# Dilated attention and a depthwise convolution on one core: the first image's loads put first, and the last image's convolution in an order of its own with diagonal products on TensorE

## The chip, the cores and the metric

The kernel runs on one core of a Trainium2 chip. The metric is the device time of one execution in microseconds (us); a change of the time by less than about 0.2% can't be told from none. Engines are named as the profile names them: PE is TensorE (its weight loads are PEld), DVE is VectorE, ACT is ScalarE, POOL is GpSimd and SP is SyncE, which here only issues transfers.

## The reference

The input is 16 images of 56 x 56 pixels with 384 channels, in single precision. Two residual layers are computed, each on a group normalisation with 32 groups of 12 channels:

```python
def _dilate_attention(q, k, v, head_dim, kernel, dil):
    ...
    attn = jnp.einsum('bgdn,bgdkn->bgnk', qg, ku) * scale
    attn = jax.nn.softmax(attn, axis=-1)
    out = jnp.einsum('bgnk,bgdkn->bgnd', attn, vu)
...
# --- layer 0 (conv_preact) ---
x = x + _L0_conv_ref(_gn(x), L0_conv_w_qkv, L0_conv_w_proj, L0_conv_b_proj)
# --- layer 1 (conv_preact) ---
x = x + _L1_conv_ref(_gn(x), L1_conv_w)
```

Layer 0 projects to q, k and v, splits the channels into 3 groups of 128 (4 heads of 32) with dilation 1, 2 and 3, lets every pixel attend to its 3 x 3 dilated neighbours, and projects back. Layer 1 is a depthwise 3 x 3 convolution with weights of -1, 0 or 1.

## The kernel before

**Chunks.** An image is worked in 7 chunks of 8 rows (448 pixels), channels on the partitions in three tiles of 128. There are N = 112 chunks, and each passes three stages. `plan_a` (L489) loads x, turns it with TensorE transposes (L510), copies it out on ACT (L523), takes statistics on DVE (L525) and stores it as `xd`. `plan_b` (L544) is layer 0: it normalises, projects (L562), scores (L627 on DVE, L608 on PE), takes the softmax, weighs (`weigh`, L686: products on DVE at L706, sums over neighbours on POOL at L716, 128 x 1344 elements each), and projects out (L737), then takes the statistics of the result (L747) and stores it as `x1d` (L750). `plan_c` (L774) is layer 1 and writes the output.

**Layer 1** treats its three channel tiles differently. Tile 0 (`column(0)` and `convolve(0)`): ACT writes the centre tap and an offset into a PSUM bank (L850), and DVE adds the eight other taps, one instruction each (L874). Tile 1: ACT likewise, but six taps are done by PE as eight products of diagonal matrices with three rows stacked on 96 partitions (L863), and two taps stay on DVE. Tile 2 (`taps_g`, `sum_g`): ACT multiplies nine times (L937), POOL adds (L947, L952, L955). For the last image alone tile 2 runs wholly on DVE instead, in nine instructions (`taps_last`, L928). Then `turn` (L958) transposes the chunk back on PE (L964), ACT copies (L970) and a transfer stores it (L973).

**Statistics.** The convolution of an image can't start before the statistics of its whole layer 0 are there. `group_norm` (L375) is a chain from DVE to PE to DVE to PE to DVE to POOL to PE to DVE to POOL to PE to DVE, with a yield at each handover. It is run for layer 0 of image 0 at the very start, and for layer 1 of image 15 at the end.

**What sets the order.** Every piece of work is filed under a number (`at`, `put`), in units where a chunk is 9 steps (`STEP`); pieces are emitted in the order of these numbers, read from the table `WHEN`. `pin` ties each instruction to the one before it on its engine while `FROM <= when < UNTIL`, that is from 81 to 1022. Outside of this stretch a scheduler fills in instructions as it thinks them ready, in emission order where it has a choice. So both ends of the program, the first image's loads and all that is filed at 1022 or later (the last image's convolution with the four chunks of image 14 before it), are ordered by the scheduler. The start files the x loads under -200 (`FIRST`), the projection weights under the same number on ACT's queue (`load_weights`, L251), and the turning of these weights between the chunks of x (`turn_qkv_weights`, L288). The small weights come in twelve transfers of single 4-byte elements and one of the bias, on SP's queue (L275, L277, L284). Constants for selections and padding are built on POOL before anything else, and a PE product of two of them (`pz`, L221) stands ahead of the transposes on PE.

**Buffers around the change.** x of image 0 is loaded into one `xin` buffer and two `z` buffers, so three chunks are under way at once. In layer 1 the tiles 0 and 1 of a chunk lie in `x1` (two buffers); a buffer comes free when `turn` has transposed it, and the next load into it is issued on SP (L835).

Of the kernel before, what the change touches and what calls it, by code (L numbers as in the profile page):

```python
# [17 lines left out]
P = 128  # L18
# [48 lines left out]
C_SHIFT = 0  # L67
FIXED_ENGINES = ("PE", "DVE", "Activation", "Pool", "SP")
# [3 lines left out]
def dilated_attention_then_binary_conv(  # L72
# [61 lines left out]
    nc.gpsimd.memset(sel, 0.0)  # L134
    for h in range(HEADS):
        nc.gpsimd.memset(sel[h * HD : (h + 1) * HD, SEL0 + h : SEL0 + h + 1], 1.0)


    perm = const.tile([P, NPAD, HEADS], F32, name="perm")
    nc.gpsimd.memset(perm, 0.0)  # L140
    for p in range(NPAD):

        v = place(p) if p < NG * NTAP else p
        nc.gpsimd.affine_select(
            out=perm[:, v, :], in_=perm[:, v, :], compare_op=ALU.not_equal, fill=1.0,
            base=-(32 * (p % 4) + 4 * (p // 4)), pattern=[[-1, HEADS]], channel_multiplier=1,
        )
# [20 lines left out]
    nc.gpsimd.memset(own, 1.0)  # L168
    for lo, s in ((-GN_G, 1), (GN_G + 3, -1)):
        nc.gpsimd.affine_select(  # L170
            out=own, in_=own, compare_op=ALU.is_ge, fill=0.0, base=lo, pattern=[[-4 * s, PARTS]], channel_multiplier=s,
        )
# [36 lines left out]
    nc.gpsimd.memset(to_pack, 0.0)  # L209
    for q in range(NQ):  # L210
        g0, c0, own_rows = (CB * NQ + q) * HD // GN_CH, GN_G + 4 * q, slice(q * HD, (q + 1) * HD)
        for g in range(NG):
            nc.gpsimd.tensor_copy(gsel[:, g, c0 : c0 + 4], gsel[:, g, g0 : g0 + 4])
        nc.gpsimd.tensor_copy(packed[own_rows, c0 : c0 + 4], gsel[own_rows, CB, g0 : g0 + 4])
    for q in range(P // HD):
        nc.gpsimd.affine_select(
            out=fold, in_=fold, compare_op=ALU.not_equal, fill=1.0, base=-q * HD,
            pattern=[[0, P // HD], [-1, HD]], channel_multiplier=1,
        )
    pz = ps_mt.tile([P, 512], F32, tag="mt", name="pz")  # L220
    nc.tensor.matmul(pz[:, :P], packed, fold.rearrange("p a c -> p (a c)"), start=True, stop=True)  # L221
    nc.vector.tensor_copy(gselz, pz[:, :P])
# [3 lines left out]
    for which, slots in enumerate((K_SLOTS, V_SLOTS)):  # L226
        kv.append([])
        for g, d in enumerate(DIL):
            kv[which].append([])
            for s in range(slots):  # L230
                t = const.tile([P, ROWS + 2 * d, W + 2 * d], F32, name=f"{'kv'[which]}_{g}_{s}")
                nc.gpsimd.memset(t[:, :, 0:d], 0.0)
                nc.gpsimd.memset(t[:, :, W + d : W + 2 * d], 0.0)
                kv[which][g].append(t)
# [3 lines left out]
    nc.gpsimd.memset(ew, 0.0)  # L238
    nc.gpsimd.memset(e3, 0.0)


    zg = []
    for s in range(2):
        t = const.tile([P, ROWS + 2, W + 2], F32, name=f"zg_{s}")
        nc.gpsimd.memset(t, 0.0)
        zg.append(t)


    raw = {}

    def load_weights():  # L251
        by_rows = w_qkv.rearrange("(t p) c -> p t c", p=P)
        for k in range(NG):
            raw["q", k] = t = t_p.tile([P, 3, PX], F32, tag="t", name="wq_in")
            nc.scalar.dma_start(t[:, :, :C], by_rows[:, 3 * k : 3 * k + 3, :])
        raw["p"] = t = w_p.tile([P, 3, PX], F32, tag="w", name="wp_in")
        nc.scalar.dma_start(t[:, :, :C], w_proj.rearrange("(t p) c -> p t c", p=P))
# [43 lines left out]
    def small_weights():  # L301
# [15 lines left out]
        nc.vector.tensor_copy(spread, spread_f)  # L317
# [167 lines left out]
    cs1 = {}  # L485
# [3 lines left out]
    def plan_a(m, t0):  # L489
# [17 lines left out]
        def turn(j):  # L507
            pt = ps_mt.tile([P, 512], F32, tag="mt", name="pt_x")
            for s in range(NSUB):
                nc.tensor.transpose(  # L510
                    pt[:, s * SUB : (s + 1) * SUB], had["xin"][:, s, j * P : (j + 1) * P], ident[:SUB, :SUB]
                )
            if b == 0:

                if j == 0:
                    pool, tag = ((xn_p, "xn"), (xn_p, "xn"), (xn_p, "xn"), (xr_p, "xr"), (t_p, "t"), (w_p, "w"),
                                 (w_p, "w"))[c]
                    first[c] = pool.tile([P, NG, PX], F32, tag=tag, name="x_first")
                xa = first[c][:, j]
            else:  # L520
                xa = xa_p.tile([P, PX], F32, tag="xa", name="xa")
            yield
            nc.scalar.copy(xa, pt[:, :PX])  # L523
            yield
            nc.vector.bn_stats(stats0[b][:, j, c, :], xa)  # L525
            yield
            if b:
                nc.sync.dma_start(xd[b][j * P : (j + 1) * P, c * PX : (c + 1) * PX], xa)
            elif j == NG - 1:
                nc.scalar.dma_start(chunk_of(xd[b], c), first[c])  # L530

        if b == 0:
            at(FIRST + 2 * max(c - 2, 0) + .14, load)
            for j in range(NG):
                at(FIRST + 2 * c + 1.11, lambda j=j: [None for _ in turn(j)])
            return
# [7 lines left out]
    def plan_b(m, t0):  # L544
# [141 lines left out]
        def weigh(i):  # L686
# [29 lines left out]
            nc.gpsimd.tensor_tensor(w0, w0, w, ALU.add)  # L716
# [47 lines left out]
    def column_scalars(b):  # L764
# [7 lines left out]
        cs1[b] = cs  # L772

    def plan_c(m, t0):  # L774
# [58 lines left out]
        def load_x():  # L833
            had["x1"] = x1 = x1_p.tile([P, JG, ROWS + 2, W], F32, tag="x1", name="x1")
# [5 lines left out]
        def column(j):  # L840

            x1, cs = had["x1"], cs1[b]
            had["pc", j] = pc = ps_q.tile([P, 512], F32, tag="q", name="pc")
# [11 lines left out]
        def convolve(j):  # L855
# [22 lines left out]

            if j >= CB:
# [3 lines left out]
                yield  # L883
            else:
# [10 lines left out]
        def load_g():  # L895
            if b < B - 1:
# [23 lines left out]
        def taps_last(ky):  # L920
# [4 lines left out]
            acc = rows(had["m"][:, 0])  # L925
            for kx in range(3):
# [48 lines left out]
        if b == B - 1:  # L975

            t0 += max(0, WHEN["statistics"][0][-1] + 1.1 - 36)
            at(t0 - 12 + .14, load_g)
            at(t0 - 3 + .14, load_x)
            ahead = 8 if c > 1 else 1  # L980
            at(t0 - ahead + .13, normalise_g)
            for j in range(JG):
                if j == CB:
                    at(t0 - 12 + j + .14, lambda: [None for _ in load()])
                    at(t0 - ahead + j + .13, lambda: [None for _ in normalise_z()])
                at(t0 + 1 + j + .05, lambda j=j: column(j))
                at(t0 + 1 + j + .05, lambda j=j: [None for _ in convolve(j)])
            for ky in range(3):
                at(t0 + 1 + ky + .05, lambda ky=ky: taps_last(ky))
            for s in range(NSUB):  # L990
                at(t0 + 12.12, lambda s=s: [None for _ in turn(s)])
# [5 lines left out]
        put(t0, "taps", taps_g)  # L997
        put(t0, "sums", lambda n: sum_g(n + 1))
# [10 lines left out]
    FROM, UNTIL = 9 * STEP, STEP * N + 14  # L1009
    at(FIRST + .14, load_weights)  # L1010
    for cc in range(NG):
        at(FIRST + 6 + 2 * cc + .12, lambda cc=cc: turn_qkv_weights(cc))
        at(-21 + cc + .12, lambda cc=cc: turn_proj_weights(cc))
    at(-18 + .14, load_small_weights)
    for o in range(NTAP):
        at(-17 + o + .14, lambda o=o: load_taps(*divmod(o, 3)))
    at(5.14, small_weights)
# [6 lines left out]
    at(FIRST + 8.125, open_banks)  # L1024
# [19 lines left out]
    earliest = min(WHEN["normalise"])[0]  # L1044
    statistics(earliest - 11, [(0, 0)], steps)
    statistics(STEP * NCH + earliest - 3, [(0, 1)], steps)
    for b in range(B):
# [26 lines left out]
    for when in sorted(pieces):  # L1074
        newest["pinned"] = FROM <= when < UNTIL
        for piece in pieces[when]:
            piece()
            pin(FIXED if newest["pinned"] else ())
# [28 lines left out]
```

## Time and profile before

| what | value |
|---|---|
| median of 3 runs | 4941.43 us (4940.76 to 4943.64) |
| the profiled execution, its own time | 4940.53 us |
| its span, first to last instruction | 4938.8 us |
| busy: PE / DVE / POOL / ACT | 4768.9 / 4423.9 / 4226.9 / 2705.6 us |
| mean granted PE clock | 0.978 |
| first projection of layer 0 starts | 56.29 us |
| last statistics input of layer 1 ends (L747) | 4781.2 us |
| statistics of layer 1, image 15, ready (L444) | 4839.8 us |

The page divides the span into 40 slices of 123.5 us; a digit is the busy share of an engine in tenths, and the row PEclk is the clock that PE was granted in tenths of full speed. A row of a timeline is: start, duration, engine, line, operation, out<-in, count, and in brackets the idle time before it and what ended it. The chain of waits is followed back from the last instruction; its rows are start, duration, and what the time went to.

### The profile page before, as it was taken

What the parts mean: (1) busy time and instruction counts of PE and PEld (TensorE: products, weight loads), DVE (VectorE), ACT (ScalarE), POOL (GpSimd) and SP (SyncE); (2) the same over time, 40 slices, a digit from 0 to 9 for tenths busy, and PEclk for the clock granted to TensorE, in tenths of its full rate; (3) what the DMA queues carried; (4) which work ended last, traced back from release to release, by engine and by line L of the source; (5) the groups of instructions that cost most, each with busy time, mean ns of one, the idle gap of its engine ahead of it and who ended that gap; (6) DMA issues with size and microseconds to landing.
All of it is one profiled execution on the core that took longest, in us unless ns stands there. A gap on an engine that the chain in (4) does not pass through costs nothing. (4 is left out here: it accounts for less than half of the span.)

```text
span 4938.8 us, 67211 instructions
## 1 busy us (share of the span) xinstructions
PE 4768.9 (97%) x22571; PEld 2204.8 (45%) x22571; DVE 4423.9 (90%) x4738; ACT 2705.6 (55%) x4952; POOL 4226.9 (86%) x2903
## 2 busy tenths in 40 slices
PE   7999999999999999999999999999999999999954
PEld 4444444444444444444444444444444444444422
DVE  4888899999999999999999999999999999989867
ACT  3332355555555555555555555655555555555565
POOL 2776798999999899998989999899999989999981
PEclk9999999999999999999999999999999999999975
DMA  5433455555555555555555555555555555544454
GB/s 163 131 108 113 134 166 165 161 166 150 166 160 164 164 161 167 153 166 154 164 165 159 168 158 166 165 162 166 150 166 160 164 163 161 160 123 133 120 152 120
DMA packets 765216, 759.93 MB, mean 154 GB/s; under 512 B 356931, under 2 KB 734150, under 8 KB 764870
## 3 DMA queue, kind: packets, MB, share of 16 engines
q1 hardware_dynamic: 756886, 743.64, 53.3%
q10 hardware_dynamic: 7984, 12.00, 0.7%
q8 instruction: 178, 2.92, 0.3%
q14 instruction: 168, 1.38, 0.1%
HBM read 401.27 MB, written 231.21 MB: 128 GB/s over the span
## 5 line engine op out<-in xcount | busy, mean ns | idle before, releaser
L716 POOL TENSOR_TENSOR w<-w 128x1344 f32<-128x1344 f32 x672 | 2050.6, 3051 | 346.1 <-DVE w L706 334.8
L706 DVE TENSOR_TENSOR w<-pb_a,v 128x1344 f32<-128x1344 f32 x1008 | 1557.8, 1545 | 230.2 <-PE pb_a L695 150.7
L627 DVE TENSOR_TENSOR t<-pq,k 128x1344 f32<-128x1344 f32 x1008 | 1513.7, 1547 | 108.9 <-PE pq L562 103.2
L562 PE MATMUL pkv<-xn,wqkvT 128*128 128x448 f32 x3924 | 1584.1, 549 | 2.6 <-DVE var L416 2.6
L562 PEld LDWEIGHTS pkv<-xn,wqkvT 128*128 128x128 f32 x3924 | 719.7, 190 | 673.7 <-issue 630.3
L737 PE MATMUL po<-y,wprojT 128*128 128x448 f32 x2016 | 845.8, 556 | 2.4 <-ACT po L733 2.4
L562 PE MATMUL pq<-xn,wqkvT 128*128 128x448 f32 x1962 | 803.5, 545 | 2.1 <-DVE x L874 1.8
L608 PE MATMUL ps<-t,sel 128*32 128x448 f32 x6048 | 656.1, 543 | 12.1 <-DVE t L627 12.0
L874 DVE SCALAR_TENSOR_TENSOR pc<-x,cs,pc 128x440 f32<-128x440 f32 (+3 forms) x896 | 598.7, 670 | 72.8 <-ACT pc L850 31.9
L947 POOL TENSOR_TENSOR m<-m 128x1344 f32<-128x1344 f32 x210 | 640.9, 3052 | 9.5 <-ACT m L937 9.2
L937 ACT ACTIVATE m<-zg,ktap 128x448 f32<-128x448 f32 x945 | 563.2, 661 | 9.7 <-POOL w L716 0.4
L523 ACT COPY xa<-pt_x 128x448 f32<-128x448 f32 x315 | 167.5, 532 | 639.1 <-PE pt_x L510 618.2
L737 PEld LDWEIGHTS po<-y,wprojT 128*128 128x128 f32 x2016 | 358.6, 191 | 300.2 <-issue 287.0
L562 PEld LDWEIGHTS pq<-xn,wqkvT 128*128 128x128 f32 x1962 | 355.2, 190 | 306.7 <-issue 304.0
L575 ACT COPY k<-pkv 128x448 f32<-128x448 f32 x336 | 179.6, 535 | 440.0 <-PE pkv L562 440.0
L719 POOL TENSOR_TENSOR y<-w 128x448 f32<-128x448 f32 x336 | 382.0, 1137 | 25.9
L720 POOL TENSOR_TENSOR y<-y,w 128x448 f32<-128x448 f32 x336 | 381.8, 1136 | 26.1
L695 PEld LDWEIGHTS <-spread 24*128 24x128 bf16 x3024 | 100.8, 91 | 650.9 <-issue 632.4
L695 PE MATMUL pb_a<-aT,spread 24*128 24x448 bf16 x3024 | 368.6, 359 | 23.5 <-DVE w L706 23.1
L575 ACT COPY v<-pkv 128x448 f32<-128x448 f32 x336 | 180.4, 537 | 330.9 <-PE pkv L562 230.1
L608 PEld LDWEIGHTS ps<-t,sel 128*32 128x32 f32 x6048 | 181.3, 109 | 322.9 <-issue 280.5
L850 ACT ACTIVATE pc<-x,cs 128x8 f32<-128x8 f32 (+7 forms) x576 | 288.6, 502 | 61.0 <-DVE t L627 24.4
(151 smaller groups left out, 4710.0 us busy)
## 6 DMA issues: line engine op xcount, KB each, us to landing
xr<-xd SPq DMA_DIRECT2D x112, 672.0 KB, 4.3
x1d<-xr SPq DMA_DIRECT2D x112, 672.0 KB, 5.3
xn<-xd SPq DMA_DIRECT2D x109, 672.0 KB, 5.6
xin<-in_x_dram SPq DMA_DIRECT2D x105, 672.0 KB, 4.7
xd<-xa SPq DMA_DIRECT2D x315, 224.0 KB, 4.3
out_dram<-osb SPq DMA_DIRECT2D x420, 168.0 KB, 3.1
z<-x1d SPq DMA_DIRECT2D x285, 224.0 KB, 3.9
x<-x1d SPq DMA_DIRECT2D x80, 560.0 KB, 4.2
```

The costliest lines, as they stand in the source:

```text
L562: nc.tensor.matmul(dst[:, :PX], wqkvT[:, cc, o0 : o0 + P], had["xn"][:, cc, :], start=(cc == 0), stop=(cc == NG - 1))
L608: return nc.tensor.matmul(had["ps"][32 * j : 32 * j + 32, :PX], sel[:, s0 : s0 + 32], tk, start=(issued[j] == 1), stop=(issued[j] == len(r ...
L627: nc.vector.tensor_tensor(t.rearrange("p k (r w) -> p k r w", w=W), q3, k3, ALU.mult)
L695: return nc.tensor.matmul(pb[:, kx, :PX].rearrange("p (s n) -> p s n", s=NSUB), spread[rows_of, v % 2, :], had["a"][rows_of, :, v // 8, :] ...
L706: nc.vector.tensor_tensor(w.rearrange("p k (r w) -> p k r w", w=W), pb[:, :, :PX].rearrange("p k (r w) -> p k r w", w=W), three(kv[1][g][m ...
L716: nc.gpsimd.tensor_tensor(w0, w0, w, ALU.add)
L719: nc.gpsimd.tensor_tensor(y, w0[:, 0], w0[:, 1], ALU.add)
L720: nc.gpsimd.tensor_tensor(y, y, w0[:, 2], ALU.add)
L737: return nc.tensor.matmul(po, wprojT[:, g, j * P : (j + 1) * P], had[f"y{g}"], start=False, stop=(g == NG - 1), skip_group_check=True,)
L874: nc.vector.scalar_tensor_tensor(acc if to is None else to[:, r0:r1], x1[:, r0 + ky : r1 + ky, x0 + kx - 1 : x_end + kx - 1], cs[:, j, 0, ...
L937: nc.scalar.activation(rows(t[:, kx]), zp[:, ky : ky + ROWS, kx : kx + W], AF.Copy, scale=ktap[:, JG, o : o + 1])
L947: nc.gpsimd.tensor_tensor(had["m"], had["m"], t, ALU.add)
```

## The change

Four things are done. (1) **Start.** The weight loads move from ACT's queue to SP's, behind the x loads; the stores of image 0's chunks move from ACT's to SP's queue, behind the weights; the small weights come after three of these stores; most constants and `pz` are built later (`late_constants`); the projection weights are turned between the steps of the first statistics; and SP, PE and DVE are pinned to this order. (2) **Last chunk of layer 0:** three of the six large additions go from POOL to DVE (`BY_VECTOR_TOO`). (3) **Image 14's** chunks 2 to 6: tile 2 of the convolution goes from ACT and POOL to DVE. (4) **Image 15:** its statistics are filed at 33 in place of 48.6 to 61.3; its convolution gets a fixed order with two steps per chunk, pinned from `LAST`; six of the eight DVE taps of tile 0 become products with diagonal matrices on PE, built once on ACT from identity (`open_diagonals`); x1 takes turns between its own two buffers and two of `z`, and the third tile's input likewise has more buffers.

```diff
+BY_VECTOR_TOO = [(1, 1), (1, 4), (1, 7)]
+END = 14
+STATS_AT = 3
+BY_DIAGONAL = ((0, 0), (1, 0), (2, 0), (0, 2), (1, 2), (2, 2))
+LATER = 6.5
+ORDER = (.2, .21, .22, .23)
+BY_VECTOR = (2, 3, 4, 5, 6)
+WEIGHTS_AT, STORE_AT, TURN_AT, LATE_AT, SMALL_AT, SMALL_USED, HEAD_ENGINES = 8.15, (20, 20.1, 20.2, 40, 40.1, 40.2, 40.3), (-3.56, -3.55, -3.24, -1), -0.05, -170, 5.14, ("SP", "PE", "DVE")
...
+    def late_constants():
...
+        pz = ps_mt.tile([P, 512], F32, tag="mt", name="pz")
+        nc.tensor.matmul(pz[:, :P], packed, fold.rearrange("p a c -> p (a c)"), start=True, stop=True)
+        nc.vector.tensor_copy(gselz, pz[:, :P])
...
-            nc.scalar.dma_start(t[:, :, :C], by_rows[:, 3 * k : 3 * k + 3, :])
+            nc.sync.dma_start(t[:, :, :C], by_rows[:, 3 * k : 3 * k + 3, :])
...
-        nc.vector.tensor_copy(spread, spread_f)
+        nc.gpsimd.tensor_copy(spread, spread_f)
...
-            elif j == NG - 1:
-                nc.scalar.dma_start(chunk_of(xd[b], c), first[c])
...
+            at(FIRST + STORE_AT[c], lambda: nc.sync.dma_start(chunk_of(xd[b], c), first[c]))
...
-            nc.gpsimd.tensor_tensor(w0, w0, w, ALU.add)
+            adder = nc.vector if (N - m, i) in BY_VECTOR_TOO else nc.gpsimd
+            adder.tensor_tensor(w0, w0, w, ALU.add)
...
+    def open_diagonals():
...
+        for n, (ky, kx) in enumerate(BY_DIAGONAL):
+            o = 3 * ky + kx
+            nc.scalar.activation(diagonals[b][:, n], ident, AF.Copy, scale=cs1[b][:, 0, 0, o : o + 1])
...
-            had["x1"] = x1 = x1_p.tile([P, JG, ROWS + 2, W], F32, tag="x1", name="x1")
+            if b < B - 1 or c % 2 == 0:
+                x1 = x1_p.tile([P, JG, ROWS + 2, W], F32, tag="x1", name="x1")
+            else:
+                x1 = z_p.tile([P, NQ * PX], F32, tag="z", name="x1_last")[:, : JG * (ROWS + 2) * W]
...
+            def whole(n):
+                ky, kx = BY_DIAGONAL[n]
...
+                return nc.tensor.matmul(
+                    pcr[:, r0:r1, x0:x_end], diagonals[b][:, n],
+                    x1[:, r0 + ky : r1 + ky, x0 + kx - 1 : x_end + kx - 1], start=False,
+                    stop=(n == len(BY_DIAGONAL) - 1), skip_group_check=True,
+                )
...
+            begin = STEP * (N - 1) + WHEN["statistics"][0][-1] + LATER
+            e = begin + 2 * c
...
+            before = e - 3.88 if c > 1 else begin - 12 + c
+            at(before, lambda: [None for _ in load()])
+            at(before + .01, load_g)
+            at(before + .02, load_x)
...
+                g_at, z_at, c_at, d_at = ORDER
+                at(e - 2 + g_at, normalise_g)
+                at(e - 2 + z_at, lambda: [None for _ in normalise_z()])
+                at(e - 2 + c_at, lambda: column(0))
+                at(e - 2 + d_at, lambda: column(1))
+            at(e + .1, lambda: go(0))
+            at(e + .11, lambda: go(1))
             for ky in range(3):
-                at(t0 + 1 + ky + .05, lambda ky=ky: taps_last(ky))
+                at(e + .4 + .01 * ky, lambda ky=ky: taps_last(ky))
+            at(e + .45, lambda: go(0))
+            at(e + .46, lambda: go(1, 2))
             for s in range(NSUB):
-                at(t0 + 12.12, lambda s=s: [None for _ in turn(s)])
+                at(e + 2.3, lambda s=s: [None for _ in turn(s)])
...
+        if b == B - 2 and c in BY_VECTOR:
+            put(t0, "taps", taps_last, [[stages[-1]] for stages in WHEN["taps"]])
+        else:
+            put(t0, "taps", taps_g)
+            put(t0, "sums", lambda n: sum_g(n + 1))
...
+    LAST = STEP * (N - 1) + WHEN["statistics"][0][-1] + LATER - 1.9
...
+    at(FIRST + WEIGHTS_AT, load_weights)
     for cc in range(NG):
...
+        at(earliest - 11 + TURN_AT[cc], lambda cc=cc: turn_qkv_weights(cc))
...
+    last = max(row[-2] for row in WHEN["out_project"]) + STATS_AT
+    statistics(STEP * (N - 1), [(1, B - 1)], [[
+        min(steps[0], last), *[last + .03 * k for k in range(len(steps) - 1)]
+    ]])
...
-        newest["pinned"] = FROM <= when < UNTIL
+        newest["pinned"] = FROM <= when < UNTIL or when >= LAST
         for piece in pieces[when]:
             piece()
-            pin(FIXED if newest["pinned"] else ())
+            pin(FIXED if newest["pinned"] else HEAD_FIXED if when < FIRST + HEAD else ())
```

## The prediction

> **What bounds the kernel now.** I read the page first, for the middle: PE is busy 97% of the span at nearly full clock, DVE 90%, and only the first and the last three of the 40 slices are thin.
>
> ```profile
> PE   7999999999999999999999999999999999999954
> DVE  4888899999999999999999999999999999989867
> POOL 2776798999999899998989999899999989999981
> PEclk9999999999999999999999999999999999999975
> ```
>
> The change touches the ends alone; the middle, ordered as before, should only shift. So a microsecond off either end is one off the total, and I read the ends.
>
> **The start**, in the timeline of the first 60 us, then in the same stretch cut into short windows:
>
> ```profile
> 14.84 0.80 PE L221 MATMUL pz<-to_pack 128*128 128x128 f32 x2 [14.84 <-POOL to_pack L216]
> ...
> 17.51 4.96 SPq L284 DMA_DIRECT2D small<-in_L_conv_w_dram  x9
> ...
> 22.59 0.59 SPq L505 DMA_DIRECT2D xin<-in_x_dram  x1
> ...
> 54.24 0.16 DVE L444 COPY mr<-pp 128x6 f32<-128x6 f32 x1 [5.10 <-PE pp L436]
> ...
> 56.29 1.70 PE L562 MATMUL pq<-x_first,wqkvT 128*128 128x448 f32 x2
> ```
>
> ```profile
> 12.50:15.00 2.50, 0.16 (x1) 0.17 (x1) 0.00 (x0) 0.00 (x0) 2.50 (x27) 1.00 1.10 317
> 15.00:17.50 2.50, 2.50 (x13) 2.28 (x14) 0.81 (x2) 0.87 (x2) 2.50 (x11) 1.00 1.14 202
> 17.50:20.00 2.50, 2.50 (x15) 2.11 (x13) 1.99 (x4) 1.26 (x3) 2.50 (x12) 1.00 0.47 3
> ```
>
> PE first waits 14.8 us for a constant that no transpose needs. The fourth chunk of x is issued only at 22.59, behind the small weights in SP's queue, while the transfers move 3 GB/s (last column) from 17.5 to 20. Statistics are done at 54.24, and the projections, from which PE never rests, begin at 56.29.
>
> **The end**, in the windows, then in the chain of waits:
>
> ```profile
> 4720.00:4760.00 40.00, 21.24 (x75) 8.31 (x75) 25.96 (x27) 19.82 (x35) 38.90 (x22) 0.63 0.52 145
> ...
> 4800.00:4820.00 20.00, 9.01 (x37) 4.28 (x37) 7.09 (x12) 16.49 (x33) 13.84 (x11) 0.50 0.61 173
> ...
> 4900.00:4920.00 20.00, 8.60 (x40) 4.04 (x44) 17.51 (x31) 7.96 (x17) 0.15 (x1) 0.50 0.40 120
> ```
>
> ```profile
> 4887.26 4.89 DMA x<-x1d
> 4892.23 1.37 ACT pc L850 x2
> 4893.65 3.16 PE pc L863 x16
> 4896.81 0.41 PE pt_o L964
> ...
> 4899.17 4.91 DMA x<-x1d
> ```
>
> The columns are PE, PE loads, DVE, ACT, POOL, then PE's clock. POOL binds to 4760; ACT and POOL hand tile 2 of image 14 to each other at 4800, where DVE is a third busy; image 15 (from 4840) is DVE's at 17.5 of 20, on a loop through the x1 load: a load is issued when `turn` frees a buffer, every 12.5 us (4862.09 to 4911.99 in four steps).
>
> **Part 1, the start.** *x.* A load landing alone took 5.4 us (the least of the ten). Chunk 0 is issued at 0.8 and lands at 6.2. A chunk's transposes free its buffer in 2.0 us (timeline: 36.04 to 37.9), so chunk 3 goes out at 8.2 and lands at 13.6; chunk 6 goes out at 15.6, in chunk 3's buffer, and lands at 21.0. From chunk 6's first transpose to its last `bn_stats` took 3.3 us (41.27 to 44.57), the aggregate 0.3: 24.6, against 45.0 now. That is -20.4. The bytes (4.8 MB at the windows' 314 GB/s, 15.3 us) don't bind; the buffers do. *Queues.* The projection weights (4 x 576 KB) move from ACT's queue behind chunk 6 on SP's. With chunk 6 ahead of them, the three that are needed first are 2.5 MB, 7.8 us from about 18 (the first bytes move 2.5 us after an issue): there at 26, when they are wanted, 2 us behind the aggregate. The stores are behind them and the small weights behind three stores; they occupied SP 14.6 us at L277 and L284, now while the statistics run. Behind them wait the last four stores, to about 36 (17.6 and 18.2 of issuing); the first reader of these is a load issued at 88.8 now, so that is covered. If DVE meets the small weights' work ahead of the statistics, it is not: second rival. *Weights turned.* 18 of 27 transposes now stand on PE between pb and pv. Nine at low clock took 2.43 us (L298), so 4.9, less the 0.8 gap that is there: +4.1. The last nine and `open_banks` (2.4 + 2.6) lie under POOL's Newton steps, a 4.1 us wait (L436): +0.9. `pz` is behind pp and needs POOL's constants, which POOL, idle 20 us now ahead of L404, can build meanwhile: 0, or at worst 2 for twelve copies (1.8, L213). The cast of `spread` (0.28, L317) goes to an idle POOL: 0. First projection 56.29 - 20.4 + 5.0 = 40.9: **-15.4** (bounds -4 and -21).
>
> **Part 2, the last chunk's additions.** Three additions leave POOL (3.05 each, L716: -9.2). Chunk 2 of image 14 also leaves one 3.05 addition fewer ahead of the last sums. But DVE, 26.0 of 40 us busy, gets three additions with both inputs in SBUF. The trace has none; I bound one by 0.6 (L667, a third of the size) and 3.05 (POOL's), and take 1.55, as L706 of the same size. It also gets nine taps of chunk 2 (5.4). That fills 10 of its 14 idle us. DVE, then nearly full, becomes the bound, and I take a third of POOL's 12.2, **-4**: the last L747 ends at 4777 (bounds 4771 and 4781). A contention shows already: L771, 220 ns in the median, took 447 beside DVE's L823, L770 367 instead of 222. The Trainium skill ("SBUF — State Buffer", Who interferes with whom) says that a DVE instruction with two SBUF inputs and a GpSimd one that reads SBUF exclude each other for their whole length; by it the three additions would give 4.6 of the 9.2 back, while with ports of their own nothing.
>
> **Part 3, image 14's last four chunks.** Tile 2's 9 ACT multiplications (0.66) and POOL's two large and three small additions (3.05 and 1.13) become 9 DVE instructions of 0.595 (spacing of L928 and L874 rows). DVE then has 19 of them per chunk, 11.3 us; with 1 us for the x1 load's handover 12.3, where sums now end every 14.2 (4778.4 to 4835.2). 4777 + 49 = 4826; image 15 starts at about 4840 now. Filed at 33, its statistics (9.4 us from aggregate to mr in the start) run beside this; if not, the last rival applies.
>
> **Part 4, image 15.** *DVE:* 19 instructions become 13: 7.7, and 0.5 for L823: 8.2. *PE:* six products of 128 x 448. A projection's is two instructions, whose weight loads (L562 from 60.10 on) are 0.375 apart: 4.5 at full clock; at half clock twice that (two L562 in 1.70), 9. L863's sixteen are 1.68 at full clock (4659.02) and 3.16 here, the twelve transposes 2.0 (paced by ACT's four copies of 0.48) and 3.1. Sum 8.2 or 15.2. I take full clock, since PE now has work all through: at half it would be busy without a rest, and in the start the rows reach 0.38 apiece within 2 us of work. The Trainium skill ("TensorE: Matmul & The Clock Gate", What's actually happening) says that half is the default and some 3.4 us of sustained work lifts it, an idle window brings it back. By that rule an x1 stall would cost PE its clock; the sum would be the fourth rival's. *ACT:* 0.85 + 2.05 + 0.28 + 1.43 + 0.71 + 4 x 0.48 = 7.2, transfers issued aside. The load loop goes: four x1 buffers, loaded two chunks ahead. `open_diagonals`, six small ACT operations (0.3 each, between L790's 0.28 and L850's 0.36), lies under DVE's work for chunk 6. Three engines at 7.2 to 8.2, each in fixed order, with handovers: I take 9.8 per chunk (bounds 8.3 and 15.2). 4826 + 68.6 + 6.5 (4932.3, the last DVE end now, to the span's end 4938.8) = 4901.1: **-37.7**.
>
> **Sum.** -15.4 - 37.7 = -53.1. The profiled execution took 4940.5 (1.7 about its span), giving 4887.4; it lies 0.9 under the median shown: **4888**.
>
> **The rivals.**
> 1. *Better:* DVE alone paces both parts: 4777 + 45.2 + 58 + 6.5 = 4886.7, -52, and the start gives -18: **4871**. For it: DVE's rows at 4857 to 4866 have no gap. Against: three nearly equal engines seldom overlap fully. Chance 0.16.
> 2. *Start mostly lost* (small weights ahead of the statistics on DVE, late constants, or weights late): -4 in place of -15.4: **4900**. For it: DVE waited 6.4 us for the small weights before (L323). Against: SP's own order puts them after everything. Chance 0.17.
> 3. *Slower:* the order makes image 15 serial. In PE's queue `turn` stands behind the next chunk's products, which wait for ACT, whose L850 for tile 1 waits for DVE's last tap of two chunks before. If nothing overlaps, a chunk is ACT 5.3 + PE 12.2 + four taps 2.4 + turn 3.1 = 23.0, and the end 4826 + 161 + 6.5, less the start's 15.4: **4981**. It decides from 17.4 per chunk on, (4938.8 + 15.4 - 6.5 - 4826) / 7. Against: banks alternate by three and by two, so a chunk of slack is there. Chance 0.03.
> 4. *PE at half clock* all through: 15.2 per chunk, 4826 + 106.4 + 6.5, tail unchanged: **4926**; half of the chunks, 4907. For it: the clock is 0.50 in most windows after 4800. Chance 0.13.
> 5. *It doesn't do what it says at the end:* the statistics stay late, image 15 starts at 4840: **4902**. Chance 0.04.
>
> **How the numbers follow.** My forecast (4876 to 4899) has 0.47, the rivals as given. The range 4862 to 4916 takes in the forecast, rivals 1, 2 and 5 and the milder half of 4, about 0.85 of the chance; it leaves out the full half clock and the serial case. Faster by over 0.2% (about what a measurement can tell from no change) 0.95, within it 0.02, slower 0.03.
>
> **What would show it.** First projection near 41, first transpose near 6, chunk 6's last `bn_stats` near 24; pv 4 us later behind pb; last L747 near 15 + 4 us earlier than now; in image 15 diagonal products 0.75 apart in pairs at a granted clock near 1.0, x1 loads issued more than a chunk ahead, DVE over 80% busy. I'm wrong if the middle doesn't shift as one, if the clock row stays at 0.50, or if DVE's order holds a stall in the first statistics.

## The result, and the profile after

The changed kernel takes 4902.5 us (median of 4 runs, 4898.35 to 4904.77) against 4942.0 for the kernel before beside it: 0.992 of its time, 95% interval 0.9906 to 0.9933. The profiled execution took 4898.35 us, its span is 4896.4. The forecast was 4888, so the sign and nearly three quarters of the gain were right, and 11 us (profiled execution) to 15 us (medians) of it didn't come. The time lies above the forecast's own band, 4876 to 4899, and within the wider range.

The slices first (rows as in the prediction). The first slice of DVE went from 4 to 6 and its last two from 67 to 88, PE's last two from 54 to 66, and the clock's from 75 to 77.

```profile
PE   8999999999999999999999999999999999999966
DVE  6888899999999999999999999999999999989988
...
PEclk9999999999999999999999999999999999999977
```

The start, in the timeline of the changed kernel (start, duration, engine, line, operation):

```profile
6.16 2.61 PE L520 MATMUL pt_x<-ident,xin 112*128 112x112 f32 x12 [6.16 <-DMA xin<-in_x_dram]
...
16.06 0.31 SPq L515 DMA_DIRECT2D xin<-in_x_dram  x1
...
30.85 0.80 PE L420 MATMUL pv<-dev,gsel 128*128 128x1 f32 x6 [0.25 <-ACT wqkvT L303]
...
37.14 0.16 DVE L454 COPY mr<-pp 128x6 f32<-128x6 f32 x1 [4.97 <-PE pp L446]
...
38.75 1.70 PE L571 MATMUL pq<-x_first,wqkvT 128*128 128x448 f32 x2
```

PE begins when the first chunk of x lands, chunk 6 is issued at 16.06 (forecast 15.6), and the projections begin at 38.75 in place of 56.29. From there the two traces run side by side: the stores of `x1d` come 16.6 to 17.9 us earlier all through the middle.

The end, in windows (length, then busy time of PE, PE loads, DVE, ACT and POOL, then PE's clock, share and GB/s of the transfers), and in the timeline:

```profile
4760.00:4780.00 20.00, 11.50 (x66) 7.75 (x68) 8.32 (x20) 7.77 (x17) 3.67 (x19) 0.70 0.54 164
4780.00:4800.00 20.00, 9.05 (x44) 2.93 (x36) 19.91 (x34) 11.95 (x22) 0.29 (x2) 0.50 0.60 167
...
4820.00:4840.00 20.00, 16.43 (x71) 7.75 (x71) 11.10 (x18) 13.70 (x27) 0.00 (x0) 0.85 0.63 157
4840.00:4860.00 20.00, 17.04 (x84) 8.08 (x85) 19.25 (x31) 14.01 (x26) 0.00 (x0) 1.00 0.79 236
```

```profile
4776.50 0.17 DVE L454 COPY mr<-pp 128x14 f32<-128x14 f32 x1 [5.63 <-PE pp L449]
...
4813.74 2.67 ACT L880 ACTIVATE pc_last<-x,cs 128x54 f32<-128x54 f32 x6 [2.01 <-DMA x<-x1d]
...
4815.38 0.68 DVE L979 SCALAR_TENSOR_TENSOR m<-zg,ktap,xg_last 128x448 f32<-128x448 f32 x1
...
4816.35 1.84 ACT L791 ACTIVATE diagonals<-ident,cs 128x128 f32<-128x128 f32 x6
...
4821.99 0.68 PE L1015 MATMUL pt_o<-ident,x 128*112 128x128 f32 x2 [6.21 <-ACT osb L1021]
4822.67 6.04 PE L913 MATMUL pc_last<-x,diagonals 128*128 128x385 f32 x12
...
4830.30 0.63 DVE L904 SCALAR_TENSOR_TENSOR pc_last<-x,cs,pc_last 128x392 f32<-128x392 f32 x1 [8.48 <-ACT pc_last L880]
```

The row at 4776.50 (`mr`) is the end of image 15's statistics, the one at 4815.38 DVE's first tap of image 15. DVE is full in image 14's rest (19.91 of 20) and in image 15 (19.25), and there are two holes: 4760 to 4780, while image 15's statistics pass (DVE 8.32 of 20), and 4820 to 4840, while image 15 opens (11.10). In the second, DVE's tap waited 8.48 us; the row names ACT, but ACT's copy into that bank had long been done: it was PE's first diagonal products, which stood behind a turn of image 14, which stood behind a copy (`osb`) that ACT had put after image 15's whole opening, in which the first column had waited 2.01 us for x1.

### The profile page after: what moved, and what is told of

The parts are those of the page before. It is cut to its first block, busy times and chain, and to the rows that moved or that the text cites. A ratio compares the mean times of both kernels' runs of the same rounds, so it can differ in the third digit from the quotient of the medians.

```text
span 4896.4 us, 67303 instructions
## 1 busy us (share of the span) xinstructions
PE 4781.9 (98%) x22655; PEld 2211.0 (45%) x22655; DVE 4435.0 (91%) x4743; ACT 2685.2 (55%) x4913; POOL 4172.3 (85%) x2876
## 5 line engine op out<-in xcount | busy, mean ns | idle before, releaser
L998 POOL TENSOR_TENSOR m<-m 128x1344 f32<-128x1344 f32 x200 | 610.3, 3051 | 0.0
L904 DVE SCALAR_TENSOR_TENSOR pc<-x,cs,pc 128x440 f32<-128x440 f32 (+1 forms) x844 | 564.6, 670 | 43.9 <-issue 13.9
L988 ACT ACTIVATE m<-zg,ktap 128x448 f32<-128x448 f32 x900 | 535.9, 661 | 12.2 <-POOL zg L954 2.7
L755 ACT COPY xr<-po 128x448 f32<-128x448 f32 x336 | 179.2, 533 | 237.6 <-PE po L747 232.0
```

Source lines behind the costliest of these rows:

```text
L904: nc.vector.scalar_tensor_tensor(acc if to is None else to[:, r0:r1], x1[:, r0 + ky : r1 + ky, x0 + kx - 1 : x_end + kx - 1], cs[:, j, 0, ...
L988: nc.scalar.activation(rows(t[:, kx]), zp[:, ky : ky + ROWS, kx : kx + W], AF.Copy, scale=ktap[:, JG, o : o + 1])
L998: nc.gpsimd.tensor_tensor(had["m"], had["m"], t, ALU.add)
```

## The experiments

All times are medians; a ratio is to the kernel before in the same series. Its interval is about 0.13% to each side, some 6 us, so smaller differences between two variants are read from the traces. For that the table cuts every profiled execution, one for each kernel, at three marks: the start of the first chunk's last L757 `bn_stats` (153.25 in the changed kernel), of the last one ahead of the last four chunks (4625.68 there), and of the last one of layer 0 (4761.32). "Start" runs from 0 to the first mark, "end" from the last mark to the span's end.

| kernel | median, us | ratio (95%) | start | middle | last four chunks of layer 0 | end |
|---|---|---|---|---|---|---|
| before | 4942 | 1 | 170.18 | 4472.86 | 137.54 | 158.2 |
| after | 4902.5 | 0.9906 to 0.9933 | 153.25 | 4472.43 | 135.64 | 135.1 |
| head_only | 4924.8 | 0.9955 to 0.9979 | 154.90 | 4471.80 | 137.92 | 158.0 |
| tail_only | 4917.3 | 0.9940 to 0.9965 | 171.69 | 4472.62 | 136.40 | 135.2 |
| no_diagonals | 4927.6 | 0.9962 to 0.9982 | 155.92 | 4471.71 | 138.03 | 162.4 |
| diagonals_only | 4924.4 | 0.9951 to 0.9978 | 154.06 | 4472.12 | 137.69 | 158.8 |
| stats_late | 4899.5 | 0.9901 to 0.9928 | 155.41 | 4470.49 | 136.49 | 131.9 |
| no_vector_adds | 4906.6 | 0.9913 to 0.9940 | 157.62 | 4472.19 | 139.29 | 135.5 |
| no_vector_taps | 4903.1 | 0.9907 to 0.9934 | 155.64 | 4472.33 | 134.62 | 139.8 |
| x1_first | 4901.1 | 0.9905 to 0.9932 | 156.92 | 4472.41 | 135.44 | 135.3 |
| open_early | 4899.2 | 0.9900 to 0.9927 | 154.98 | 4471.82 | 135.84 | 134.2 |
| both_ends | 4892.6 | 0.9889 to 0.9916 | 155.63 | 4472.02 | 135.29 | 127.8 |
| weights_first | 4904.2 | 0.9909 to 0.9936 | 160.72 | 4469.48 | 135.23 | 135.1 |
| stores_early | 4911.9 | 0.9925 to 0.9953 | 169.01 | 4471.69 | 136.23 | 135.1 |

### The start's part and the end's part

`head_only` is the kernel before with the start's edits alone, `tail_only` with all the others:

```diff
# head_only, against the kernel before (the main lines)
-            nc.scalar.dma_start(t[:, :, :C], by_rows[:, 3 * k : 3 * k + 3, :])
+            nc.sync.dma_start(t[:, :, :C], by_rows[:, 3 * k : 3 * k + 3, :])
...
+            at(FIRST + STORE_AT[c], lambda: nc.sync.dma_start(chunk_of(xd[b], c), first[c]))
...
+    at(earliest - 11 + LATE_AT, late_constants)
...
+            pin(FIXED if newest["pinned"] else HEAD_FIXED if when < FIRST + HEAD else ())
# tail_only, against the kernel before (the main lines)
+            adder = nc.vector if (N - m, i) in BY_VECTOR_TOO else nc.gpsimd
...
+                in_one_go([lambda n=n: whole(n) for n in range(len(BY_DIAGONAL))])
...
+            begin = STEP * (N - 1) + WHEN["statistics"][0][-1] + LATER
...
+        if b == B - 2 and c in BY_VECTOR:
...
+        newest["pinned"] = FROM <= when < UNTIL or when >= LAST
```

> Kernel before with the start's edits alone (x first on SP, weights and stores behind it, constants and pz late, PE, DVE and SP in fixed order in the first stages). Theory, from the two traces: every later store of image 0 and on comes 16.9 to 17.65 us earlier, so the start is worth 17.4 us wherever the end stands: 4941.5 - 17.4 = 4924, ratio 0.9965. Rival 'the start is mostly lost' (the prediction's second): what is late next eats it, 4936 to 4941. Rival 'the parts help each other' (the tail can use the earlier start better): 4928 to 4934.

> Kernel before with everything but the start's edits (three additions and image 14's taps on VectorE, early statistics, fixed pipeline with diagonals). Theory, additive: the profiled after-run ends 157.6 - 134.5 = 23.1 us nearer to the last bn_stats, and the additions give 1.9: 4941.5 - 25 = 4916.5; by the medians (39.4 in all, less 17.4) 4919.5. Rival 'the parts hinder each other': more than 25 us alone, below 4914. Rival 'the end works only with the new start': above 4924.

Measured: 4924.8 and 4917.3, that is -17.0 and -24.6 beside the kernel before. The sum, -41.6, is the whole change's -39.4 within the intervals. The parts add up: the start is worth about 17 and the end about 24, and neither needs the other. In the table the start's edits show in the first column alone, the end's in the last two.

### Diagonal products without the pipeline, pipeline without the products

```diff
# no_diagonals
-BY_DIAGONAL = ((0, 0), (1, 0), (2, 0), (0, 2), (1, 2), (2, 2))
+BY_DIAGONAL = ()
...
-                in_one_go([lambda n=n: whole(n) for n in range(len(BY_DIAGONAL))])
...
-                at(begin - 1.83, open_diagonals)
# diagonals_only, against head_only (the main lines)
+            elif b == B - 1:
+                in_one_go([lambda n=n: whole(n) for n in range(len(BY_DIAGONAL))])
+                yield
+                for ky, kx in ((0, 1), (0, 0), (1, 0), (2, 0), (0, 2), (1, 2), (2, 2)):
+                    if (ky, kx) not in BY_DIAGONAL:
+                        tap(ky, kx)
...
+                if c == 0 and j == 0:
+                    at(t0 + .9, open_diagonals)
```

> The changed kernel without the diagonal products: in image 15 the six taps of column half 0 go to VectorE again, in the same fixed pipeline, and the six diagonal matrices are not made. Theory: VectorE (19.25 of 20 us busy in the steady stretch) becomes the only bound, with six taps of 0.69 us more per chunk: period 9.4 to about 13.1, 7 chunks, less about 4 us of opening (diagonals and first products at half clock): 4902 + 26 - 4 = 4924. Rival 'TensorE's products set the period and VectorE would fill its gaps': under +8, 4902 to 4910. Rival 'the diagonals brought everything of the end's gain': 4925 or more, with image 15 as long as in the kernel before.

> The kernel with the start's edits alone, and of the end's only the diagonal products: in image 15 six products take the place of six VectorE taps of column half 0, at the taps' old places in the order; additions, image 14's taps, statistics, buffers and the order of image 15 as in the kernel before. Theory (the diagonals carry the end's gain, 25 us between the changed kernel with and without them): 4924.8 - 25 = 4900, no more than 5 beside the changed kernel's 4902. Rival 'the products need the fixed pipeline': without it VectorE's, ScalarE's and TensorE's shares of a chunk stand in line and half of the gain or less is left, 4912 to 4925.

Measured: 4927.6, in the range of the second rival (4925 or more) and not told apart from the theory's 4924 by the time; and 4924.4, where the theory said 4900 and the rival 4912 to 4925. Without the products the pipeline's end is 4 us longer than before the change (162.4 against 158.2), and without the pipeline the products bring nothing (158.8); the whole change's end is 23 shorter. `diagonals_only` also lacks image 14's taps on DVE and the early statistics; by the experiments below the taps are worth 4.7 of the 23 and the early statistics cost some 3, so they don't account for the difference. So "the diagonals carry the gain" was half a sentence. What the pipeline alone lacks is DVE time. In the timeline of `no_diagonals`, two chunks of image 15:

```profile
4845.54 4.98 DVE L904 SCALAR_TENSOR_TENSOR pc_last<-x_last,cs,pc_last 128x448 f32<-128x448 f32 x7
...
4859.25 4.98 DVE L904 SCALAR_TENSOR_TENSOR pc_last<-x,cs,pc_last 128x448 f32<-128x448 f32 x7
```

The period is 13.71 us in place of 9.41, and the 4.3 between them is six taps at the 0.72 us at which they follow each other. What the products alone lack is a chunk that is there. In `diagonals_only`, a window, and the transfer and the tap on either side of a hole:

```profile
4860.00:4880.00 20.00, 12.29 (x61) 5.73 (x54) 9.59 (x17) 10.09 (x21) 0.00 (x0) 0.74 0.60 189
```

```profile
4863.51 0.38 SPq L853 DMA_DIRECT2D x<-x1d  x1
...
4871.49 0.69 DVE L962 SCALAR_TENSOR_TENSOR m<-zg,ktap,xg_last 128x448 f32<-128x448 f32 x1 [8.55 <-ACT zg L949]
```

DVE is busy 9.59 of 20. The x1 load goes out at 4863.51, just behind PE's turns of the chunk that held the buffer (4861.02 on). ACT's column of that chunk starts at 4869.97, 0.08 us after the load has landed by the trace, `zg` stands behind it on ACT at 4870.62, and DVE idles 8.55 us until 4871.49. That is the loop through the x1 load that the prediction saw in the kernel before, at about its old length (from 4840.39 to 4889.32 there are four loads, 12.2 us for each): relieving DVE doesn't shorten it. The buffers and the order together take the loop away (which of the two does it was not tried), and then DVE's own time counts.

### The statistics of image 15

```diff
# stats_late
-    statistics(STEP * (N - 1), [(1, B - 1)], [[
-        min(steps[0], last), *[last + .03 * k for k in range(len(steps) - 1)]
-    ]])
-    for b in range(B - 1):
+    for b in range(B):
```

> The changed kernel with image 15's statistics back at their old place in the order (48.6 to 61.3 steps after the last chunk's start instead of 33), the rest unchanged. The chain is serial (14.7 us from the last bn_stats to mr in the changed kernel, with VectorE 8.3 of 20 us busy in that window). Theory A: the stall is paid wherever the chain stands, only moved, and nothing else waits for it: 4900 to 4905. Theory B (the one I hold): late, it also holds image 15's first column, diagonals and products, which now start 52 us after the last bn_stats while mr came 59 us after it before: 4909 to 4917. Theory C: late, the chain falls where VectorE has image 14's work to do and the stall goes away: 4888 to 4894.

Measured: 4899.5; the end is 131.9 instead of 135.1. Theory B, which I held, is wrong: `mr` comes 34 us later and image 15's first tap into a bank (`pc_last`) doesn't (4830.30 in the changed kernel):

```profile
4810.81 0.17 DVE L454 COPY mr<-pp 128x14 f32<-128x14 f32 x1 [0.16 <-PE pp L449]
...
4828.21 0.63 DVE L904 SCALAR_TENSOR_TENSOR pc_last<-x,cs,pc_last 128x392 f32<-128x392 f32 x1 [7.66 <-ACT pc_last L880]
```

Late, the chain finds image 14's work ready on DVE: its wait for `pp` is 0.16 us instead of 5.63, its three waits together 3.3 instead of 8.1, and DVE is busy 50.0 us from 4760 to 4820 instead of 47.4. By the time alone theory A (4900 to 4905) would do as well; the end and these rows speak for theory C in kind, though not for its 8 to 14 us. Filing these statistics early, all in one go, bought nothing and cost about 3 us.

### DVE's share of attention's last chunk and of image 14

```diff
# no_vector_adds
-BY_VECTOR_TOO = [(1, 1), (1, 4), (1, 7)]
+BY_VECTOR_TOO = []
# no_vector_taps
-BY_VECTOR = (2, 3, 4, 5, 6)
+BY_VECTOR = ()
```

> The changed kernel with its three last additions of attention back on GpSimd (3.05 us each there, 3.42 beside VectorE's work, against 1.54 on VectorE). Theory, from the two traces: they brought 1.9 us of the time up to the last bn_stats, so 4902 + 2 = 4904. The prediction's price: + 4, 4906. Rival 'they brought nothing' (the end with the tail alone has its last bn_stats at 4780.7, the kernel before at 4780.6; the slower additions are hidden by VectorE's other work): 4900 to 4903.

> The changed kernel with image 14's chunks 2 to 6 convolved over column group 2 in the old way (nine ScalarE taps, GpSimd's sums) instead of nine taps on VectorE of 0.68 us each. Theory: after the last bn_stats VectorE is full from 4779.8 to 4814.5 and four or five chunks of it carry 6.1 us of those taps; ScalarE (12 of 20 us busy there) and GpSimd (idle there) could take them, but the old way costs ScalarE 9 x 0.68 per chunk more and its sums three GpSimd operations on the path to each chunk's end: about the same, 4898 to 4908. Rival 'VectorE is the bound of image 14's rest': five times 6.1 us fall away on VectorE, 4875 to 4890. Rival 'GpSimd and ScalarE were the bound of the kernel before there': 4912 or more, most of what the end gained beyond the diagonals.

Measured: 4906.6, +4.1, and 4903.1, +0.5. The time alone doesn't settle either; the table says more. The last four chunks of layer 0 take 139.3 without the additions on DVE, 135.6 with them: 3.7. Without image 14's taps on DVE they take 134.6: those taps cost 1.0 there and give 4.7 at the end (139.8 against 135.1). Each figure is one profile: other kernels with both edits take 135.2 to 136.5 there, and `no_diagonals` 138.0, for which no cause was found, so the 3.7 is rough. The price of the additions is in the timeline of the changed kernel, DVE and POOL:

```profile
4721.32 3.04 POOL L726 TENSOR_TENSOR w<-w 128x1344 f32<-128x1344 f32 x1 [1.50 <-DVE w L726]
4723.26 2.50 DVE L726 TENSOR_TENSOR w<-w 128x1344 f32<-128x1344 f32 x1
4724.43 2.33 POOL L729 TENSOR_TENSOR y<-w 128x448 f32<-128x448 f32 x1
...
4740.09 1.54 DVE L726 TENSOR_TENSOR w<-w 128x1344 f32<-128x1344 f32 x1
```

The same DVE addition takes 1.54 when POOL rests (at 4740.09), and POOL's small one 1.13. Here DVE's ends 1.40 after POOL's addition ends, and POOL's next ends 1.00 after DVE's: they took turns.

### The opening of image 15

```diff
# x1_first
-            if b < B - 1 or c % 2 == 0:
+            if b < B - 1 or c % 2:
                 x1 = x1_p.tile([P, JG, ROWS + 2, W], F32, tag="x1", name="x1")
# open_early: this, and
+OPEN_AHEAD = 5
...
-                at(begin - 1.85, normalise_g)
+                at(begin - OPEN_AHEAD, normalise_g)
...
# both_ends: both, and
-        min(steps[0], last), *[last + .03 * k for k in range(len(steps) - 1)]
+        min(steps[0], last), *[last + when - steps[1] for when in steps[1:]]
```

> The changed kernel with the two places for x1 of image 15's chunks exchanged: chunk 0 (and 2, 4, 6) loads into a z buffer, free at about 4799, chunk 1 (and 3, 5) into an x1 buffer, free at 4809. Theory: column 0, which waited 2.0 us for that load at 4813.7 after ScalarE's zg, starts that much earlier, and the diagonals, the osb copies, TensorE's turns (6.2 us of wait) and the first products with it: - 2, 4900. Rival 'the load is what VectorE's 8.5 us of idle are made of': - 6 or more, below 4896. Rival 'the next wait takes its place' (osb's buffers, SP held 15 us by the output stores): 0 to - 1, 4901 to 4903.

> As x1_first, and ScalarE's opening of image 15 (zg, column 0, diagonals, z, column 1) ordered 3.15 of 9 steps earlier, ahead of the osb copies of image 14's last two chunks. Theory: the first products no longer wait behind those copies, the 8.5 us in which VectorE is idle at 4822 shrink to 1 to 3: 4893 to 4897. Rival 'it only moves the wait' (image 14's osb copies and turns are now behind the opening, VectorE idles ahead of it): 4899 to 4905. Rival 'half clock': the products take 6.0 us instead of 4.7 wherever they stand, so of the 8.5 at most 7 can go: not told apart from the theory by the time alone, but by the products' duration.

> As open_early (x1 places exchanged, ScalarE's opening of image 15 ordered 3.15 steps earlier), and the statistics of image 15 spread over the 6.9 of 9 steps that they have elsewhere, beginning where the changed kernel begins them. Theory: the serial chain leaves other work between its links, VectorE's idle time of some 11 us after the last bn_stats falls to about 6 as with the late statistics: 4899.2 - 4 = 4895, ratio 0.9905. Rival 'VectorE lacks work there whatever the order' (image 14's chunks wait for transfers and ScalarE): 4898 to 4901, with the same idle time under other names.

Measured: 4901.1, 4899.2 and 4892.6. `x1_first` starts column 0 1.9 us earlier after the last `bn_stats` (50.5 instead of 52.4), and the end stays at 135.3: DVE still idles 7.38 us instead of 8.48, for the first products now run at half clock for longer (7.04 us instead of 6.04) and give back half of it. That is the rival of the next wait, though the wait is another one than it named. `open_early` shrinks the hole as forecast, and opens another, so that its rival is right as well. The timeline of `open_early`:

```profile
4784.07 0.69 DVE L980 SCALAR_TENSOR_TENSOR m<-zg,ktap,xg 128x448 f32<-128x448 f32 x1 [5.45 <-ACT zg L962]
...
4829.02 0.63 DVE L905 SCALAR_TENSOR_TENSOR pc_last<-x_last,cs,pc_last 128x392 f32<-128x392 f32 x1 [2.02 <-ACT pc_last L881]
```

8.48 became 2.02, but DVE waits 5.45 us for `zg` at 4784, behind the statistics. In `both_ends` that wait is 0.42 and the hole of the opening stays closed; a window and a row of its timeline:

```profile
4760.00:4780.00 20.00, 14.42 (x81) 8.62 (x79) 12.85 (x29) 10.90 (x23) 3.67 (x19) 0.74 0.53 147
```

```profile
4822.96 0.63 DVE L905 SCALAR_TENSOR_TENSOR pc_last<-x_last,cs,pc_last 128x392 f32<-128x392 f32 x1 [2.13 <-ACT pc_last L881]
```

`mr` is there no sooner (14.7 us from the end of the last `bn_stats`, as in the changed kernel), but DVE is busy 12.85 us in this window instead of 8.32 (13.2 instead of 8.6 in the 20 us from the end of each kernel's last `bn_stats`): spread over 6.9 steps, the chain lets other work between its links. The end takes 127.8, 7.3 less. By its median this kernel is 49 us below the kernel before and 10 below the changed one; the intervals of the two ratios overlap slightly, and the table's last column carries the difference.

### The start: bytes and queues

```diff
# weights_first
-            nc.sync.dma_start(t[:, :, :C], by_rows[:, 3 * k : 3 * k + 3, :])
+            nc.scalar.dma_start(t[:, :, :C], by_rows[:, 3 * k : 3 * k + 3, :])
...
-    at(FIRST + WEIGHTS_AT, load_weights)
+    at(FIRST + .14, load_weights)
# stores_early
-            at(FIRST + STORE_AT[c], lambda: nc.sync.dma_start(chunk_of(xd[b], c), first[c]))
+            at(FIRST + 2 * c + 1.115, lambda: nc.scalar.dma_start(chunk_of(xd[b], c), first[c]))
```

> The changed kernel with the weights (2.36 MB) issued at the start from ScalarE's queue again, ahead of x, the stores of image 0 still late. The changed kernel moved 4.8 MB of x in 21.3 us, about 225 GB/s. Theory (x waits for bytes that go ahead of it): the weights take 10 us of the transfers, chunk 6's transposes come at 31 instead of 21.3, first projection at 47 to 49 instead of 38.75, less up to 3 for weights turned earlier: 4902 + 8 = 4910. Rival 'the stores alone held x': transposes of chunk 6 by 23, 4901 to 4904.

> The changed kernel with image 0's stores of x (0.69 MB a chunk) issued from ScalarE's queue again as soon as a chunk is turned, weights still behind x. Theory: each store shares the transfers with the chunks still to come; some five of the seven, 3.4 MB, fall into the loading of x at 225 GB/s: chunk 6's transposes at 30 to 36 instead of 21.3, first projection at 46 to 53, 4909 to 4916. Rival 'the weights alone held x': chunk 6 by 23, first projection within 1 of 38.75, 4901 to 4904.

Measured: 4904.2 (+1.7) and 4911.9 (+9.4). With the weights first, chunk 6's transposes come at 28.88 instead of 21.34 (the theory said 31) and the first projection at 47.37 (47 to 49), but the theory's time, 4910, didn't come: the first mark is only 5.3 us later than the mean of the ten kernels with the changed start (155.4), the middle is some 2.5 shorter, and the time moved less than it can tell. The middle may owe this to PE's clock: by the trace it falls to 0.50 for 3.41 us at some 4345 to 4364 us in twelve of the fourteen kernels, but not in `weights_first` and `stats_late`, which have the two shortest middles (4469.5 and 4470.5). Such a stretch would cost 1.7 us, an estimate from the half clock, if PE had work in all of it. The early stores have the theory's time (4909 to 4916) but not its step, transposes at 30 to 36; most of their cost came by a way that I hadn't named. The rows of PE and ACT:

```profile
26.09 2.61 PE L520 MATMUL pt_x<-ident,xin 112*128 112x112 f32 x12 [1.19 <-DMA xin<-in_x_dram]
...
34.91 0.97 ACT L533 COPY x_first<-pt_x 128x448 f32<-128x448 f32 x2 [7.28 <-DMA wp_in<-in_L_conv_w_proj_dram]
```

The bytes delay chunk 6 by 4.8 us (26.09 against 21.34). Then ACT, which has yet to make the last two copies of chunk 6 for the statistics, waits 7.28 us. The trace names the landing of a weight load; in ACT's order a store stands ahead of these copies, and it is issued at 34.51, 0.4 us before them. In the trace the program's transfers signal eight semaphores in turn, and this store has the same one as the weight load: it goes out 0.08 us after that load has landed, at 34.43. So the queue costs more than the bytes here; the first mark is 13.6 us later than the mean of the ten. That the constants and `pz` held PE, and the small weights SP, was not tried by itself.

## Why the prediction was right, and where it was not

**Right: the start.** -15.4 was forecast, `head_only` gives -17.0, the marks give -15.5 (155.4 against 170.9, the mean of the kernels with the old start). The first projection comes at 38.75 in the changed kernel's profile and at 41.5 in the mean of the ten (forecast 40.9), so 2 us of the -17.4 that this one profile shows are luck. The steps hold: chunk 0 at 6.2, chunk 6 in at 21.3 (21.0), aggregate done at 25.0 (24.6). In the chain of the statistics the product `pv` came 4.1 us behind the end of `pb` where it was 0.8 behind: +3.3, not +4.1. The +0.9 under the Newton steps didn't come, since the last nine transposes and `open_banks` took 1.7 us each at full clock, and PE still waited 1.62 us for POOL. "The bytes don't bind; the buffers do" holds as long as x goes first; with weights ahead, they bind (chunk 6 at 28.88).

**Half right: the additions.** -4 was forecast to the last `bn_stats`, with the taps of image 14 that fall there counted in; the two traces show -1.9 between the last two marks. By the table the additions alone bring 2.9 (137.5 to 134.6 in `no_vector_taps`), and image 14's taps take 1.0 back. The step that was mis-sized is "a third of POOL's 12.2". The Trainium skill ("SBUF — State Buffer", Who interferes with whom) has DVE instructions with two SBUF inputs and GpSimd's reads exclude each other. The row of 2.50 us agrees, and not all additions met a reader (the one of 1.54 didn't).

**Wrong: "its statistics run beside this".** Part 3 let 49 us pass from the last `bn_stats` to image 15 (four chunks at 12.3); it was 53.4 (4761.9 to 4815.4). The chain took 14.7 us from the last `bn_stats`, not 9.4, and DVE lost about 11 us by the waits of its rows in the chain and just behind it (0.36, 2.13, 5.63 and 3.11), because its own instructions of the chain stand in its queue and wait there. Only 4.4 of the 11 show in the sum; DVE was then nearly full (19.91 and 19.12 of 20 us in the next two windows). Rival 5 named the time, 4902, for statistics that stay late; with late statistics the time is no longer but 3 us shorter, so its agreement with the number is chance.

**Wrong: the opening of image 15.** Part 4 counted 9.8 per chunk and a drain, 75.1 us in all; from DVE's first tap to the end it was 81.0. The step that failed is "`open_diagonals` lies under DVE's work for chunk 6". The 1.84 us were right in size, but ACT did them in line with the load of x1, two columns and the z's, and the copies for image 14 came after. DVE idled 8.48 us. Three runs moved that wait about, and only the one that also gave the statistics room got it back.

**Right by two errors: 9.8 per chunk.** The steady period is 9.41. I counted 13 DVE instructions at 0.595 and 0.5 for L823, 8.2, and 1.6 of handovers. The handovers are nil (DVE is busy 19.25 of 20); it is DVE's own work that is longer, since nine taps in a row on one tile follow each other at 0.72. PE comes close: its products start when DVE's taps end, and the chain of waits shows one turn of the loop through both, 9.42 us:

```profile
4850.47 4.71 PE pc_last L913 x12
...
4858.43 0.70 DVE pc_last L904
4859.15 0.69 DVE x_last L904
4859.89 4.71 PE pc_last L913 x12
```

**The other rivals.** Half clock (rival 4) fell: the clock is 1.00 from 4840 to 4880. In image 15 it showed in the first products, 6.04 us for what takes 4.7, and in the last 5.6 us. The Trainium skill ("TensorE: Matmul & The Clock Gate", What's actually happening) puts the change after some 3.4 us of sustained work. The granted clock of the trace goes from 0.50 to 1.00 at 4825.95, 4.0 us after PE's work began at 4821.99, and in `x1_first` 6.0 after (4823.53 to 4829.51), so the rule's size fits the first better than the second. In all fourteen traces the changes of the clock lie whole multiples of 3.41 us apart (from the one before, at 4767.92, to the one at 4825.95 it is 17 of them), so when a change comes depends also on where these points lie. Serial (rival 3) fell: the steady period is 9.41, far from 17.4. A start mostly lost (rival 2) fell with `head_only`, and the better case (rival 1) with the two holes.

In sum, against the profiled execution: start -17.4 (forecast -15.4), to the last `bn_stats` -1.9 (-4), from there to image 15 4.4 us late (53.4 against 49), image 15 5.9 late (81.0 against 75.1): -2.0 + 2.1 + 4.4 + 5.9 = 10.4 of the 10.7 that the span lies over the forecast's. The medians lie further apart since the profiled execution was the shortest of the four. So the start was sized rightly, the period by luck, and what didn't come is half of the additions' gain, the time that the statistics hold DVE, and the opening of image 15.

## What to carry to other kernels

Taking work off a busy engine paid nothing here as long as a loop through a buffer set the period, and breaking the loop paid nothing as long as the engine had too much work: try the two together before calling either useless. A serial chain filed "early" in one go didn't run beside other work, for each engine takes its instructions in a fixed order; it needs that work placed between its links (7.3 us at the end in `both_ends`, with the earlier opening), and the first chunk of a pipeline needs as much care as its period. A transfer issued from a compute engine's queue can wait there for another transfer and hold the engine's own work (7.28 us in `stores_early`).

## What had not been expected of the hardware

- Nine DVE taps of 128 x 448 that accumulate in one tile follow each other at 0.72 us (seven in 5.01), alternating between two tiles at 0.59 (rows at 4850.64, 4851.23, 4851.82 of the kernel before). At 8 such pairs per chunk that is 1 us of the 9.41; a pipeline that alternates them was not run.
- Ten kernels with the same edits at the start reach the first mark between 153.25 and 157.62 us. PE's clock may be part of it: six small products for the first statistics (24.76 in the changed kernel) took 0.80 us in the changed kernel and in `diagonals_only`, which have the two earliest marks, and 1.41 in the eight others. The changed kernel's profiled run has the earliest mark of all, 2.2 us under the mean.
